# Layer 1's result turned by VectorE and stored in runs of 512 bytes, with the tokens of a block reordered, in a two-layer attention kernel

## The chip, the cores and the metric

The kernel runs on one core of a Trainium2 chip. The metric is the device time of one execution in microseconds (us); lower is better. Engines are named as the profile names them: PE (TensorE, matmuls), PEld (its weight loads), DVE (VectorE), ACT (ScalarE), POOL (GpSimd), SP (SyncE, which issues nearly all DMAs here).

## What is computed

The input x has 4 batches of 128 channels and 64 x 64 = 4096 positions, in fp32. Layer 0 is attention over the positions of a group-normalised x, with a gate and a projection, added to x. Layer 1 treats each position as a token of 128 channels: self attention with one shared projection for queries and keys, added to the tokens, and then a batch-normalised linear map that drives a recurrence over the tokens. Cut to what matters:

```python
# layer 0 (per batch; q and k have 64 rows, v and gate 128)
attn = softmax(q.T @ k * SCALE);  x = x + proj((v @ attn.T) * gate)
# layer 1
t = to_tokens(x)                                  # [B, 4096, 128]
q = ln(t) @ W;  t = t + softmax(q @ q.T) @ ln(t)
wx = batchnorm(ln(t) @ Wf.T)
y[:, i] = sigmoid(wx[:, i] + y[:, i-1] @ V.T)     # along the tokens
x = from_tokens(t + y)                            # back to [B, 128, 4096]
```

Softmax is a sum over all keys, so tokens may be kept in any order inside a block as long as scores, values and results agree on it. The recurrence and the output need them in their natural order.

## The kernel before

All work is in `fast`; `general` is another path, taken only if a check on the device fails at the end, and it isn't taken here. Batches run one after the other. A batch's 4096 tokens are 8 blocks (NB) of 512 (QB), and a block is 4 tiles (NQ) of 128 tokens.

**Layer 0** (`layer0`, run by `attention`): for each query block, 16 pairs of key tiles; TensorE makes scores (L223), ScalarE the exponential e (L225), VectorE adds e into acc for the denominators (L230, L232), and TensorE multiplies with v (L403), two pairs behind (LAG). The e tiles rotate through 4 buffers. When a block is through, `finish` queues small steps in `pending`: `sums`, `denominators`, `projection`, `tokens`, with `nothing` as empty places. The attention loop takes one step of `pending` every so many iterations, or one of `ahead` (the next batch's norms and projections), so that these steps lie between the matmuls.

Layer 0 has channels on the partitions and layer 1 has tokens there. `move` (L255) makes that turn: VectorE transposes 32x32 blocks (L261) into d, one DMA writes d (256 KB) to a DRAM scratch turn_d (L264), and four DMAs of 64 KB read it back (L266) so that the 32x32 blocks land where a full transpose has them. There are three moves in a block: x with the bias (tile t), the projected attention (yt), and the normalised tokens h (qt).

**Layer 1** (`layer1`): the score matrix is symmetric, since queries and keys are the same. For each block n (order 6, 7, 5, 4, ... 0) only blocks a <= n are computed: scores (L672), exponentials with row sums into slots (L678), and products with h (L539, in `direct`). For a < n the exponentials are also turned, by VectorE (L683) into dd and by 16 DMAs of 64 KB per pair of blocks (L710) into tt, and used four iterations later for block a (L552 in `reversed_products`), whose row sums DVE takes at L557. In the last batch the pair of blocks 1 and 0 isn't turned: block 0 computes block 1's scores itself, in the order given by `order`. `count` counts a block's parts and calls `finish` when they are complete; its limit is one lower for blocks 0 and 1 of the last batch.

`finish` (L579) loads the stored tokens (L599) and queues: `tokens` (the attention result oacc transposed on TensorE L608, scaled and added on DVE L610 to give t1, layernorm L276 to L280, with 1/sqrt on GpSimd L131, L132, to give h2), `result` (t1 transposed on TensorE L621, copied by ScalarE L624, stored to t2_d L625), two empty places, `turn` (h2 transposed on TensorE L630, copied by ScalarE L631 to th), `inputs` (the linear map L635, its statistics L636, and a copy L639 or L642). In the last batch's blocks 0 to 3 there are no empty places, and block 0's `tokens` goes to the head of the queue. These steps share one PSUM bank (ps_m).

**The scan** at the end: t2 loads all four t2_d (L776); the recurrence runs over pieces of 32 tokens with 12 tokens of warm-up, 44 steps in all, each with two matmuls (L823), two sigmoids (L827) and preloads (L810); the results are added to t2 (L837) and stored (L842).

The program's instructions are put in order on each engine by the framework's scheduler, so the order on the chip is near the order of the code but not the same.

Of the kernel before, what the change touches and what calls it, by code (L numbers as in the profile page):

```python
# [18 lines left out]
P = 128  # L19
B, C, N = 4, 128, 4096  # L20
# [9 lines left out]
QB = 512  # L30
NB = N // QB
# [18 lines left out]
def conv_attn_hybrid_kernel(  # L50
# [17 lines left out]
    turn_d = [dram.tile([P, 4, NQ, 32], F32, name=f"turn{i}_d") for i in range(8)]  # L68
    t2_d = dram.tile([B, C, N], F32, name="t2_d")
    wx_d = dram.tile([B, C, N], F32, name="wx_d")  # L70

# [86 lines left out]
def fast(  # L158
# [13 lines left out]
    with ExitStack() as st:  # L172
# [79 lines left out]
                nc.tensor.matmul(m[:, r, :cols], lhsT=lhsT[rs], rhs=rhs[rs], start=True, stop=True)  # L252
            return m[:, 0, :cols], m[:, 1, :cols]

        def move(blocks, dst):  # L255

            nonlocal n_moves
            d = work.tile([P, 4, NQ, 32], F32, tag="d", name="d", bufs=2)  # L260
            nc.vector.transpose(d.rearrange("q a j i -> q j a i"), blocks)  # L261
            via = turn_d[n_moves % len(turn_d)]
            n_moves += 1
            nc.sync.dma_start(via, d)  # L264
            for a in range(4):
                nc.sync.dma_start(dst[bass.ts(a, 32)], via[:, a].rearrange("(p i) j k -> i p j k", p=4))  # L266

        n_moves = 0

# [15 lines left out]
        def tiles(t):  # L285

            return [t[:, :, j, :] for j in range(NQ)]

        def quarters(t):
            return [t[:, j, :].rearrange("q (p i) -> q p i", p=4) for j in range(NQ)]  # L290
# [97 lines left out]
        def layer0(b, gate, q, k, v, need):  # L388
            h = big.tile([P, NT, C], F32, tag="h", name="h")
            qt = big.tile([P, N], F32, tag="qt", name="qt")  # L390

            def score_mm(n, p, half):
                r = bass.ts(half, DQ)
                return k[r, bass.ts(p, P)], q[r, bass.ts(n, QB)]

            def weigh(o, n, p, e):

                if o is None:
                    o = [ps_o.tile([P, QB], F32, tag="o", name=f"o{r}") for r in range(2)]
                for h in range(2):  # L400
                    for r in range(2):
                        rs = bass.ts(r, DQ)
                        nc.tensor.matmul(  # L403
                            o[r], lhsT=v[rs, p + h * PAIRS, :], rhs=e[rs, h, :],
                            start=(p == 0 and h == 0), stop=(p == PAIRS - 1 and h == 1),
                        )
                return o

            def finish(n, o, acc):
                cs, ts = bass.ts(n, QB), bass.ts(n, NQ)  # L410
                og = work.tile([P, QB], F32, tag="og", name="og")
# [10 lines left out]
                sub = stat.tile([P, NQ, 4], F32, tag="sub", name="sub", bufs=2)  # L422

                def sums():


                    half, blocks = acc[:, 0, :], acc[:, 1, :]
                    nc.vector.tensor_tensor(half, half, blocks, ALU.add)
                    nc.vector.transpose(blocks, half)
                    nc.vector.tensor_reduce(  # L430
                        sub, blocks.rearrange("q (j f k) -> q j f k", j=NQ, f=4), AX.X, ALU.add
                    )
                    move(xb.rearrange("c (j f k) -> c j f k", j=NQ, f=4), t)

                def denominators():
                    m0, m1 = halves(quart, sub.rearrange("q j f -> q (j f)"))
                    tot = stat.tile([P, NQ, 4], F32, tag="tot", name="tot", bufs=2)
                    flat = tot.rearrange("q j f -> q (j f)")
                    nc.vector.tensor_copy(flat, m0)
                    nc.vector.tensor_tensor(flat, flat, m1, ALU.add)  # L440
                    nc.vector.tensor_tensor(
                        tot, tot,
                        own.rearrange("q (j f) -> q j f", j=1).to_broadcast([P, NQ, 4]), ALU.mult,
                    )
                    den = den_all[:, b * NT + n * NQ : b * NT + (n + 1) * NQ]
                    nc.vector.tensor_reduce(den, tot, AX.X, ALU.add)
                    nc.vector.reciprocal(rinv, den)

                def projection():
                    m0, m1 = halves(wt["ps"], og)  # L450
                    nc.scalar.copy(og, m1)
                    nc.vector.tensor_tensor(og, m0, og, ALU.add)
                    move(og.rearrange("c (j f k) -> c j f k", j=NQ, f=4), yt)

                def tokens():
                    for j in range(NQ):
                        nc.vector.scalar_tensor_tensor(  # L457
                            t[:, :, j, :], yt[:, :, j, :], rinv[:, j : j + 1], t[:, :, j, :],
                            ALU.mult, ALU.add,
                        )  # L460
                    nc.sync.dma_start(t_d[b, n], t)
                    layernorm(tiles(t), quarters(h[:, ts, :]))

                    move(
                        h[:, ts, :].rearrange("q j (p i) -> q j p i", p=4),
                        qt[:, cs].rearrange("c (p j k) -> c p j k", j=NQ, p=4),
                    )
                    done.add((b, n))

                pending.extend([sums, nothing, denominators, projection, nothing, tokens])  # L470

            attention(score_mm, None, SCALE, weigh, finish, need)
            return h, qt

        def layer1(b, h, qt):
# [52 lines left out]
            def order(n):  # L528


                return [0, 1] if b == B - 1 and n == 0 else list(range(n, -1, -1))

            def turns(n, a):
                return a < n and not (b == B - 1 and n == 1)
# [37 lines left out]
            def count(n):  # L572


                parts[n] += 1
                if parts[n] == NB - (b == B - 1 and n < 2):
                    finish(n)

            def finish(n):  # L579
# [3 lines left out]
                if b == B - 1 and n == 0:  # L583

                    one, two = (ep.tile([P, 2, QB], F32, tag="e", name="last") for _ in range(2))
                    h2, t1 = (one[:, r, :].rearrange("q (j c) -> q j c", j=NQ) for r in range(2))
                    th, t2 = two[:, 0, :], two[:, 1, :]

                    def bank():
                        return ps_s.tile([P, 2, QB], F32, tag="s", name="ml")[:, 0, :]  # L590
                else:
                    h2 = work.tile([P, NQ, C], F32, tag="h2", name="h2")
                    th = work.tile([P, QB], F32, tag="th", name="th")
                    t1 = work.tile([P, NQ, C], F32, tag="og", name="t1b")
                    t2 = None

                    def bank():
                        return ps_m.tile([P, QB], F32, tag="m", name="m1")
# [16 lines left out]
                    layernorm(quarters(t1), quarters(h2))  # L615

                def result():
                    nonlocal t2
                    m = bank()
                    for j in range(NQ):  # L620
                        nc.tensor.transpose(m[:, bass.ts(j, P)], t1[:, j, :], ident)  # L621
                    if t2 is None:
                        t2 = work.tile([P, QB], F32, tag="xb", name="t2")
                    nc.scalar.copy(t2, m)  # L624
                    nc.sync.dma_start(t2_d[b, :, cs], t2)  # L625

                def turn():
                    m = bank()
                    for j in range(NQ):
                        nc.tensor.transpose(m[:, bass.ts(j, P)], h2[:, j, :], ident)  # L630
                    nc.scalar.copy(th, m)  # L631

                def inputs():
                    m = bank()
                    nc.tensor.matmul(m, lhsT=wt["f"], rhs=th, start=True, stop=True)  # L635
# [8 lines left out]

                if b == B - 1 and n == 0:
                    pending.appendleft(tokens)
                    pending.extend([result, turn, inputs])
                elif b == B - 1 and n < 4:
                    pending.extend([tokens, result, turn, inputs])
                else:  # L650
                    pending.extend([tokens, result, nothing, nothing, turn, inputs])


            for n in [NB - 2, NB - 1] + list(range(NB - 3, -1, -1)):
# [4 lines left out]
                for a in order(n):  # L659
# [4 lines left out]
                    for i in range(2):  # L664
# [588 lines left out]
```

## Time and profile before

| | us |
|---|---|
| three runs | 3066.79, 3070.16, 3072.19 |
| median | 3070.16 |
| the profiled execution | 3067.95, its span 3066.1 |
| PE busy | 3000.1 (98%) |
| DVE busy | 1882.3 (61%) |
| ACT busy | 1154.7 (38%) |
| POOL busy | 148.3 (5%) |
| DMA packets | 233171, 241 MB |

How to read the profile: a group's line gives source line, engine, operation, output and inputs with the shape, the count, then the busy us in total and the mean ns of one, and behind the last bar the idle time of the engine just before these instructions and what ended it. The chain of waits is the work that ended last, followed back from the end. The granted TensorE clock was full (mean 0.994) but for the first microseconds and the stretch between attention and scan.

### The profile page before, as it was taken

The numbers are of one execution on the slowest core, as the hardware profiler recorded it, in microseconds if no ns is written. First come the engines' busy times: TensorE is split into PE (matmuls) and PEld (weight loads), VectorE is DVE, ScalarE is ACT, GpSimd is POOL, SyncE is SP. The second block draws the span as 40 slices with busy tenths as digits, with TensorE's granted clock in tenths as the row PEclk, the third lists the DMA queues.
The fourth block names the chain that finished last, engine by engine and source line by source line (L and its number), as shares of the span: only waits on it lengthen the run. The fifth ranks groups of instructions, "written<-read, shape, count | busy, mean of one in ns | idle before, by whom it ended". The sixth has DMA issues, their size and how long they took to land.

```text
span 3066.1 us, 32642 instructions
## 1 busy us (share of the span) xinstructions
PE 3000.1 (98%) x10834; PEld 1377.5 (45%) x10834; DVE 1882.3 (61%) x3160; ACT 1154.7 (38%) x2148; POOL 148.3 (5%) x187
## 2 busy tenths in 40 slices
PE   7999999999999999999999999999999999999996
PEld 3444444444444444444444444444444444444443
DVE  6666665655666666655567666655566666455556
ACT  3444433333344443333344443333334444323334
POOL 0000000000000000000000000000000000000000
PEclk9999999999999999999999999999999999999998
DMA  1011143433211123333311113333321112543333
GB/s 52 28 56 56 42 115 86 99 93 92 53 56 55 41 82 96 93 96 92 85 46 61 39 50 112 88 96 93 94 61 52 46 49 90 139 104 93 99 111 159
DMA packets 233171, 241.17 MB, mean 79 GB/s; under 512 B 88480, under 2 KB 144288, under 8 KB 231968
## 3 DMA queue, kind: packets, MB, share of 16 engines
q1 hardware_dynamic: 231984, 238.18, 27.8%
q8 instruction: 89, 1.46, 0.2%
q14 instruction: 90, 0.74, 0.1%
q10 hardware_dynamic: 1008, 0.79, 0.1%
HBM read 65.80 MB, written 56.62 MB: 40 GB/s over the span
## 4 chain that ended last, share of the span: by engine, by line
PE 95%; DVE 3%; ACT 1%; POOL 0%; DMA 0%; issue 0%; ACTq 0%; SPq 0%; DVEq 0%; POOLq 0%
PE o L403 29%; PE o L539 16%; PE ps L223 15%; PE ps L672 14%; PE ot L552 12%; PE m L252 1%; PE m L635 1%; PE mq L497 1%; PE ps L505 1%; PE mp L335 1%; PE mp L370 1%; PE mp L355 1%; DVE ps_r L810 1%; DVE t2s L837 1%; PE m L630 1%; PE m L608 0%
## 5 line engine op out<-in xcount | busy, mean ns | idle before, releaser
L403 PE MATMUL o<-e,nxt 64*128 64x512 f32 x4096 | 964.8, 590 | 0.0
L225 ACT ACTIVATE e<-ps 128x1024 f32<-128x1024 f32 x512 | 521.6, 1025 | 678.2 <-PE ps L223 653.2
L232 DVE TENSOR_TENSOR acc<-acc,e 128x1024 f32<-128x1024 f32 x448 | 547.6, 1222 | 237.4 <-ACT e L225 221.6
L403 PEld LDWEIGHTS o<-e,nxt 64*128 64x128 f32 x4096 | 399.6, 187 | 483.4 <-issue 475.1
L678 ACT ACTIVATE e<-ps,shift 128x512 f32<-128x512 f32 x516 | 350.4, 683 | 670.0 <-PE ps L672 506.1
L539 PE MATMUL o<-e,h 128*128 128x512 f32 x1160 | 539.5, 592 | 0.0
L223 PE MATMUL ps<-nxt 64*128 64x512 f32 x2048 | 535.8, 597 | 2.2 <-ACT e L225 2.2
L672 PE MATMUL ps<-qt 128*128 128x512 f32 x1032 | 490.9, 595 | 2.9 <-ACT qt L498 2.7
L552 PE MATMUL ot<-tt,h 128*128 128x512 f32 x888 | 399.5, 592 | 0.0
L683 DVE STREAM_TRANSPOSE dd<-e 128x512 f32<-128x512 f32 x444 | 287.2, 687 | 87.9 <-ACT e L678 75.3
L539 PEld LDWEIGHTS o<-e,h 128*128 128x128 f32 x1160 | 218.3, 190 | 266.5 <-issue 261.9
L223 PEld LDWEIGHTS ps<-nxt 64*128 64x128 f32 x2048 | 194.4, 187 | 231.2 <-issue 158.9
L672 PEld LDWEIGHTS ps<-qt 128*128 128x128 f32 x1032 | 187.8, 190 | 213.0 <-issue 188.0
L552 PEld LDWEIGHTS ot<-tt,h 128*128 128x128 f32 x888 | 168.0, 190 | 209.5 <-issue 206.8
L557 DVE TENSOR_REDUCE slots<-tt 128x4 f32<-128x2048 f32 x111 | 250.8, 2260 | 9.8 <-DMA tt<-dd 9.2
L566 DVE TENSOR_TENSOR oacc<-oacc,ot 128x512 f32<-128x512 f32 x87 | 59.7, 686 | 187.0 <-PE ot L552 186.9
L131 POOL TENSOR_SCALAR rstd<-mv 128x4 f32<-128x4 f32 x64 | 14.5, 227 | 2429.7 <-DVE mv L277 2429.7
L678 ACT ACTIVATION_READ_ACCUMULATOR e<-ps,shift 128x1 f32 x516 | 101.3, 196 | 0.0
L457 DVE SCALAR_TENSOR_TENSOR t<-yt,rinv,t 128x128 f32<-128x128 f32 x128 | 36.6, 347 | 71.1 <-DMA yt<-turn_d 71.1
L420 POOL TENSOR_SCALAR xb<-xb,bpc 128x512 f32<-128x512 f32 x32 | 60.9, 1904 | 321.0 <-DMA xb<-in_x_dram 311.3
L132 POOL TENSOR_TENSOR rstd<-rstd,mhalf 128x4 f32<-128x4 f32 x64 | 66.4, 1037 | 5.3
L280 DVE TENSOR_SCALAR h<-t,mv,rstd 128x128 f32<-128x128 f32 x128 | 35.7, 344 | 47.0 <-POOL rstd L132 47.0
(160 smaller groups left out, 1659.5 us busy)
## 6 DMA issues: line engine op xcount, KB each, us to landing
tt<-dd SPq DMA_DIRECT2D x1776, 64.0 KB, 2.0
turn_d<-d SPq DMA_DIRECT2D x96, 256.0 KB, 2.0
t_d<-t SPq DMA_DIRECT2D x63, 256.0 KB, 2.0
nxt<-in_x_dram SPq DMA_DIRECT2D x16, 512.0 KB, 5.6
xb<-in_x_dram SPq DMA_DIRECT2D x32, 256.0 KB, 2.9
t<-turn_d SPq DMA_DIRECT2D x128, 64.0 KB, 2.0
yt<-turn_d SPq DMA_DIRECT2D x128, 64.0 KB, 2.0
qt<-turn_d SPq DMA_DIRECT2D x128, 64.0 KB, 2.1
```

The source lines that it names most:

```text
L132: nc.gpsimd.tensor_tensor(dst, dst, mhalf[:, :n], ALU.pow)
L223: nc.tensor.matmul(ps[:, h, :], lhsT=lhsT, rhs=rhs, start=True, stop=True)
L225: nc.scalar.activation(e, ps, AF.Exp, scale=scale)
L232: nc.vector.tensor_tensor(acc, acc, e, ALU.add)
L403: nc.tensor.matmul(o[r], lhsT=v[rs, p + h * PAIRS, :], rhs=e[rs, h, :], start=(p == 0 and h == 0), stop=(p == PAIRS - 1 and h == 1),)
L420: nc.gpsimd.tensor_scalar(xb, xb, bpc, None, ALU.add)
L539: nc.tensor.matmul(o, lhsT=h[:, NQ * a + 2 * i + half, :], rhs=e[:, half, :], start=(a == order(n)[0] and i == 0 and half == 0), stop=(a = ...
L552: nc.tensor.matmul(ot, lhsT=h[:, NQ * n + j, :], rhs=t[:, :, j, :, :].rearrange("q p k j -> q k p j"), start=(j == 0), stop=(j == NQ - 1),)
L557: nc.vector.tensor_reduce(slots[:, bass.ts(n, NQ), a], t.rearrange("q p b k j -> q b p (k j)"), AX.XY, ALU.add,)
L672: nc.tensor.matmul(ps[:, half, :], lhsT=qt[:, bass.ts(at, P)], rhs=qt[:, bass.ts(n, QB)], start=True, stop=True,)
L678: nc.scalar.activation(e[:, half, :], ps[:, half, :], AF.Exp, bias=shift, accum_out=slots[:, at, n : n + 1],)
L683: nc.vector.transpose(d.rearrange("q f b k j -> q k b f j")[:, 2 * i + half], e[:, half, :].rearrange("q (b f j) -> q b f j", b=NQ, f=NQ),)
```

## The change

- The order of tokens inside a block of layer 1 is another one. Tile j's partition (f, k) holds token 128f + 32j + k of the block, where it was token 128j + 32f + k. `sums`, `denominators` and `projection` follow (views `f j k` for `j f k`), and `inputs` reads th through a permuted view that puts the tokens in their natural order.
- `move` becomes `turn_out` and a read: VectorE's transpose as before, then four DMAs of 64 KB write it to DRAM in runs of 512 bytes, each from 32 partitions; the scratch turn_d then has the finished layout [128, 512], and one DMA of 256 KB reads it.
- `result` uses `turn_out` to store t1 to t2_d: a DVE transpose and four DMAs take the place of four TensorE transposes, the ScalarE copy and one DMA. It is no longer a step of its own in `pending`; `turn` calls it at its end.
- In the last batch, block 0 takes its parts in the order [1, 0] instead of [0, 1], and a part for block 1 is counted when its scores for it are issued, so block 1's `finish` is called then instead of earlier. The limits of `count` follow.

```diff
-        def move(blocks, dst):
+        def turn_out(blocks, dst):
             d = work.tile([P, 4, NQ, 32], F32, tag="d", name="d", bufs=2)
             nc.vector.transpose(d.rearrange("q a j i -> q j a i"), blocks)
+            for f in range(4):
+                nc.sync.dma_start(
+                    dst.rearrange("(a i) m -> i a m", a=4)[:, :, bass.ts(f, P)],
+                    d[bass.ts(f, 32)].rearrange("i a j k -> i a (j k)"),
+                )
+
+        def move(blocks, dst):
+            nonlocal n_moves
             via = turn_d[n_moves % len(turn_d)]
             n_moves += 1
-            nc.sync.dma_start(via, d)
-            for a in range(4):
-                nc.sync.dma_start(dst[bass.ts(a, 32)], via[:, a].rearrange("(p i) j k -> i p j k", p=4))
+            turn_out(blocks, via)
+            nc.sync.dma_start(dst, via)
...
-                return [0, 1] if b == B - 1 and n == 0 else list(range(n, -1, -1))
+                return [1, 0] if b == B - 1 and n == 0 else list(range(n, -1, -1))
...
-                if parts[n] == NB - (b == B - 1 and n < 2):
+                if parts[n] == NB - (b == B - 1 and n == 0):
                     finish(n)
...
                 def result():
-                    nonlocal t2
-                    m = bank()
-                    for j in range(NQ):
-                        nc.tensor.transpose(m[:, bass.ts(j, P)], t1[:, j, :], ident)
-                    if t2 is None:
-                        t2 = work.tile([P, QB], F32, tag="xb", name="t2")
-                    nc.scalar.copy(t2, m)
-                    nc.sync.dma_start(t2_d[b, :, cs], t2)
+                    turn_out(t1.rearrange("q j (p i) -> q j p i", p=4), t2_d[b, :, cs])
...
                     nc.scalar.copy(th, m)
+                    result()
...
-                    nc.tensor.matmul(m, lhsT=wt["f"], rhs=th, start=True, stop=True)
+                    natural = th.rearrange("c (j p k) -> c p j k", j=NQ, p=4)
+                    nc.tensor.matmul(m, lhsT=wt["f"], rhs=natural, start=True, stop=True)
...
-                    pending.extend([result, turn, inputs])
+                    pending.extend([turn, inputs])
                 elif b == B - 1 and n < 4:
-                    pending.extend([tokens, result, turn, inputs])
+                    pending.extend([tokens, turn, inputs])
                 else:
-                    pending.extend([tokens, result, nothing, nothing, turn, inputs])
+                    pending.extend([tokens, nothing, nothing, turn, inputs])
...
-                            if a == n and i == 0:
+                            if a == order(n)[0] and i == 0:
                                 direct()
+                        if a > n and i == 1:
+                            count(a)
```

More of the change, by code (lines that the diff above doesn't have):

```diff
@@ L66, in conv_attn_hybrid_kernel @@
     t_d = dram.tile([B, NB, P, 4, NQ, 32], F32, name="t_d")
-    turn_d = [dram.tile([P, 4, NQ, 32], F32, name=f"turn{i}_d") for i in range(8)]
+    turn_d = [dram.tile([P, QB], F32, name=f"turn{i}_d") for i in range(8)]
     t2_d = dram.tile([B, C, N], F32, name="t2_d")
@@ L253, in halves @@
             return m[:, 0, :cols], m[:, 1, :cols]
+        def turn_out(blocks, dst):
+            d = work.tile([P, 4, NQ, 32], F32, tag="d", name="d", bufs=2)
+            nc.vector.transpose(d.rearrange("q a j i -> q j a i"), blocks)
+            for f in range(4):
[3 more added lines that the diff above has]
+                )
         def move(blocks, dst):
             nonlocal n_moves
-            d = work.tile([P, 4, NQ, 32], F32, tag="d", name="d", bufs=2)
-            nc.vector.transpose(d.rearrange("q a j i -> q j a i"), blocks)
             via = turn_d[n_moves % len(turn_d)]
             n_moves += 1
-            nc.sync.dma_start(via, d)
-            for a in range(4):
-                nc.sync.dma_start(dst[bass.ts(a, 32)], via[:, a].rearrange("(p i) j k -> i p j k", p=4))
+            turn_out(blocks, via)
+            nc.sync.dma_start(dst, via)
         n_moves = 0
@@ L287, in tiles, with flat @@
             return [t[:, :, j, :] for j in range(NQ)]
+        def flat(t):
+            return t.rearrange("q p j i -> q (p j i)")
         def quarters(t):
@@ L420, in finish @@
                 nc.gpsimd.tensor_scalar(xb, xb, bpc, None, ALU.add)
-                sub = stat.tile([P, NQ, 4], F32, tag="sub", name="sub", bufs=2)
+                sub = stat.tile([P, 4, NQ], F32, tag="sub", name="sub", bufs=2)
                 def sums():
@@ L430, in sums @@
                     nc.vector.tensor_reduce(
-                        sub, blocks.rearrange("q (j f k) -> q j f k", j=NQ, f=4), AX.X, ALU.add
+                        sub, blocks.rearrange("q (f j k) -> q f j k", j=NQ, f=4), AX.X, ALU.add
                     )
-                    move(xb.rearrange("c (j f k) -> c j f k", j=NQ, f=4), t)
+                    move(xb.rearrange("c (f j k) -> c j f k", j=NQ, f=4), flat(t))
                 def denominators():
[L436 to L440, printed above, removed]
+                    m0, m1 = halves(quart, sub.rearrange("q f j -> q (f j)"))
+                    tot = stat.tile([P, 4, NQ], F32, tag="tot", name="tot", bufs=2)
+                    both = tot.rearrange("q f j -> q (f j)")
+                    nc.vector.tensor_copy(both, m0)
+                    nc.vector.tensor_tensor(both, both, m1, ALU.add)
                     nc.vector.tensor_tensor(
                         tot, tot,
-                        own.rearrange("q (j f) -> q j f", j=1).to_broadcast([P, NQ, 4]), ALU.mult,
+                        own.rearrange("q (f j) -> q f j", j=1).to_broadcast([P, 4, NQ]), ALU.mult,
                     )
                     den = den_all[:, b * NT + n * NQ : b * NT + (n + 1) * NQ]
-                    nc.vector.tensor_reduce(den, tot, AX.X, ALU.add)
+                    nc.vector.tensor_reduce(den, tot.rearrange("q f j -> q j f"), AX.X, ALU.add)
                     nc.vector.reciprocal(rinv, den)
@@ L452, in projection @@
                     nc.vector.tensor_tensor(og, m0, og, ALU.add)
-                    move(og.rearrange("c (j f k) -> c j f k", j=NQ, f=4), yt)
+                    move(og.rearrange("c (f j k) -> c j f k", j=NQ, f=4), flat(yt))
                 def tokens():
@@ L462, in tokens @@
                     layernorm(tiles(t), quarters(h[:, ts, :]))
[L464 to L467, printed above, removed]
+                    move(h[:, ts, :].rearrange("q j (p i) -> q j p i", p=4), qt[:, cs])
                     done.add((b, n))
@@ L586, in finish @@
                     h2, t1 = (one[:, r, :].rearrange("q (j c) -> q j c", j=NQ) for r in range(2))
-                    th, t2 = two[:, 0, :], two[:, 1, :]
+                    th = two[:, 0, :]
                     def bank():
@@ L594, in finish @@
                     t1 = work.tile([P, NQ, C], F32, tag="og", name="t1b")
-                    t2 = None
                     def bank():
```

## The prediction

> **What bounds the kernel now.** I read the page first: busy shares and the chain of work that ended last.
>
> ```profile
> span 3066.1 us, 32642 instructions
> ...
> PE 3000.1 (98%) x10834; PEld 1377.5 (45%) x10834; DVE 1882.3 (61%) x3160; ACT 1154.7 (38%) x2148; POOL 148.3 (5%) x187
> ...
> PE 95%; DVE 3%; ACT 1%; POOL 0%; DMA 0%; issue 0%; ACTq 0%; SPq 0%; DVEq 0%; POOLq 0%
> ```
>
> TensorE is busy for 98% of the span and holds 95% of the chain; no queue or DMA holds 1%. So an instruction taken off TensorE should shorten the span by what it holds, and work on another engine costs only where TensorE comes to wait for it. Next the groups of instructions, shapes kept apart, for the step that is moved (busy us, mean ns; then the engine's idle time before them):
>
> ```profile
> L261 DVE STREAM_TRANSPOSE d<-h 128x512 f32<-128x512 f32 x32 | 22.8, 711 | 1.1
> ...
> L621 PE MATMUL m<-ident,t1b 128*128 128x128 f32 x124 | 18.9, 275 | 0.0
> ...
> L624 ACT COPY t<-m 128x512 f32<-128x512 f32 x31 | 18.1, 584 | 56.0 <-PE m L621 51.5 <-issue 4.6
> ```
>
> TensorE never waited before L621 (idle 0.0): its 124 transposes (4 more, of the very last block, have a row of their own) cost array time and no wait. How much is not the 275 ns, because matmuls overlap. TensorE's timeline (start, us, group) gives it:
>
> ```profile
> 2952.27 0.60 PE L621 MATMUL m<-ident,t1b 128*128 128x128 f32 x4
> 2952.71 1.02 PE L672 MATMUL ps<-qt 128*128 128x512 f32 x2
> ...
> 2961.13 0.60 PE L608 MATMUL m<-ident,oacc 128*128 128x128 f32 x4
> 2961.57 3.60 PE L539 MATMUL o<-e,h 128*128 128x512 f32 x8
> 2965.00 0.60 PE L621 MATMUL m<-ident,t1b 128*128 128x128 f32 x4
> ```
>
> From the start of four transposes to the start of what follows is 2952.71 - 2952.27 = 0.44 us. Attention ends when the last L539 is through, at 2965.00. From there the bound changes: a serial stretch leads to the scan. The chain of waits there (start, us):
>
> ```profile
> 2965.75 0.85 DVE h L280 x3
> 2966.61 0.61 DVE oacc L566
> ...
> 2967.26 0.66 PE ml L608 x4
> ...
> 2971.43 1.05 POOL rstd L132
> ...
> 2972.90 1.11 PE ml L630 x4
> 2974.03 0.59 ACT last L631
> ...
> 2974.67 2.09 PE ml L635 x2
> ```
>
> Here VectorE carries the end: block 0's last sum (oacc) starts only when block 1's layernorm output h is done. The sigmoid that opens the scan starts at 2982.20.
>
> **What the Trainium skill says.** "Trainium Kernel Development and Optimization", Performance Expectations, calls matmul busy time a bad metric because matmuls are pipelined. The trace agrees: 0.60 us stand in the row where 0.44 us pass, so I price TensorE by distances between starts. "VectorE: DVE Perf Modes", The three transpose paths, says that VectorE turns 32x32 blocks only and writes SBUF, where TensorE turns 128x128 into PSUM. So the full turn must be finished by the addresses of the DMA, which is what the stores do; L261 has this operation at 711 ns for 128x512. "DMA: Bandwidth & Descriptors", Specifications, puts line rate at 512 B or more. Before, the runs through turn_d are 512 B on reading; after, on writing. No row shows a store in such runs.
>
> **The change part by part.**
>
> 1. *Result off TensorE.* 32 x 4 transposes go. 30 of the 32 groups start before 2965.00: 30 x 0.44 = **13.2 us** off TensorE's stream. The other two (blocks 1 and 0 of the last batch) lie beside VectorE's work in the serial stretch: nothing. The 32 copies L624 free ScalarE of 32 x 0.584 = 18.7 us; at 38% busy that is no time of the span.
>
> 2. *Turned by VectorE.* 32 transposes of 0.711 us, 22.8 us more. In a window of layer 1 (500 to 740 us) VectorE is busy 138 of 240 us, so it is hidden there. But the compiled order puts the transpose ahead of the layernorm's last aggregation, so GpSimd's 1/sqrt and the output h come 0.64 us later (start to start of such a transpose and what follows, at 137.13 and 137.77). The L630 transposes wait for h: the chain from t1 to h is 1.04 + 1.21 + 0.64 + 1.47 + 1.03 = 5.4 us. Between tokens and turn lie two empty slots, and one iteration of layer 1 (two score and two direct products) is 4 x 0.86 = 3.44 us: hidden. Only blocks 1 to 3 of the last batch have no slot between; there it may cost 0 to 1 us each, and I take nothing since the order again puts other products between.
>
> 3. *Moves.* Before: one 256 KB write, then four 64 KB reads; after: four 64 KB writes, then one 256 KB read, so five SP issues either way. In one block the write issued at 126.68, the reads at 128.71, and VectorE went on with yt at 132.23: 5.55 us. After: four issues of 0.43 (1.73 us in that block), 2.0 to land, 0.34 to issue the read, 2.9 to 3.0 to land (rows xb and t of 256 KB): about 7.0 us, 1.4 more. If a store of 512 B pieces landed at 3.0 it would be 2.4 more; at 1.8, the shortest 64 KB read, 1.2. VectorE waits in order: behind its L457 stand the acc adds L232, and ScalarE's exponentials wait for those through the four e buffers. In that block the e buffer written at 142.62 had been freed by an add that ended at 138.95, 3.7 us earlier. So 1.4 us is hidden: nothing.
>
> 4. *The store's issues.* 1 becomes 4 per block on SP, 96 more, at 0.33 to 0.63 us each. The L710 transfers queue behind them, and L552 waits for those.
>
> ```profile
> 572.44 10.00 SPq L710 DMA_DIRECT2D tt<-dd  x16
> 586.67 0.33 SPq L625 DMA_DIRECT2D t_d<-t  x1
> ```
>
> SP issues 16 in 10.0 us, and L552 groups start 12.9 us apart (593.61, 606.49, 619.43): some 2.9 us free per turn, against at most 4 x 0.63 - 0.33 = 2.2 us once per several turns. Also SP stood 142.2 us at L625 waiting for ScalarE's copy, a wait that an early VectorE transpose mostly takes away. Nothing.
>
> 5. *The last batch's end.* Block 1 is now complete only when block 0's scores for it exist. In the compiled order its four L608 transposes come after the last direct product, not before: 0.44 us more off the stream, and its whole token step lands in the serial stretch. From the last product's end (0) on VectorE: oacc 0.2 to 0.8; t1 of block 1 to 1.84; stats with the transpose among them 1.21 + 0.64, to 3.69; 1/sqrt 1.47, to 5.16; h to 6.2; three of block 0's scaled adds to 6.97. Block 1's turn on TensorE and ScalarE brings its bn_st to 8.3, through at 8.95, and the last aggregation to 9.05; 1/sqrt to **10.5**, where block 0's normalise starts. Before, that was 2972.50 - 2965.00 = 7.5: **3.0 us longer**. From there the chain is the same 9.7 us to the scan; block 0's own transpose fits where VectorE waited 2.05 us for L635. Bounds: 0 (if engines overlap as before) to 6.
>
> 6. *Orders of tokens.* L635 reads a permuted operand as L497 does: 599 against 610 ns, so nothing (62 x 11 ns = 0.7 us either way). sums and denominators keep instructions and sizes.
>
> Sum: -13.2 - 0.44 + 3.0 = **-10.6 us**, on the profiled span 3055.5. That execution took 3067.95, inside the runs' 3066.79 to 3072.19; from their median 3070.16 the forecast is **3059.6 us**.
>
> **The rivals.**
>
> *The gain is mostly given back.* The serial stretch grows by 6 instead of 3, blocks 1 to 3 hold TensorE up 1 us each, and the scan waits up to 2 us for t2s: its loads issued at 2976.82, took up to 22.4, and were first used at 3002.3, 3.1 us of margin, while block 0's store now ends some 3 us later than before. That is -13.6 + 6 + 3 + 2 = -2.6: 3067.6, no change. For it: VectorE and GpSimd take turns in that stretch. Against: L630 waited only 1.8 us in all before.
>
> *SP's queue becomes the bound in layer 1 (slower).* If nothing of the store's 2.2 us per block were hidden, that is 32 x 2.2 = 70 us; the point where it decides is 10.6 / 32 = 0.33 us per block getting through to L552. With a third getting through, +23 - 10.6: 3082.6. For it: SP is 78% taken (10.0 of 12.9 us). Against: L552 waited for tt only 2.4 us in all, and SP's 142.2 us wait falls away.
>
> *More is gained.* The serial stretch does not grow: -13.6, 3056.6.
>
> That the change does not do what it says is excluded by the compiled order: no L621 left, stores of 32x4x128.
>
> **How the numbers follow.** A measurement here tells about 0.2% (6.1 us) from no change: faster is below 3064.0, slower above 3076.3. Forecast 0.70 (3056 to 3063), more gained 0.12, given back 0.12, SP 0.06: faster 0.82, same 0.12, slower 0.06. The range, 3055.0 to 3066.5, takes in the tail's bounds, the blocks' waits, the runs' own scatter of 2.7 us and the nearer half of the give-back.
>
> **What would show it.** Right: PE's busy time down by about 19 us with L621's rows gone, L683 and L232 counts unchanged, the last direct product 13 to 14 us earlier, and 10 to 11 us instead of 7.5 from there to block 0's normalise. Wrong: L552 or L630 waiting for DMA or VectorE by more than some us in total, ScalarE's L225 waiting longer for acc than the 13.6 us of now, or the scan waiting for t2s. A slower landing than 3 us of the 64 KB stores would break step 3 first.

## The result, and the profile after

The changed kernel takes **3080.92 us** (median of 4 runs, 3079.55 to 3082.70) against 3069.86 us (3066.79 to 3072.19) beside it: a ratio of 1.0037, 95% interval 1.0020 to 1.0054. It is slower by 11 us where 10.6 us less were forecast. The profiled spans, 3078.5 and 3066.1 us, differ by 12.4 us; the sum of the prediction had said 3055.5, so 23.0 us are to be explained.

The page of the kernel after:

```profile
span 3078.5 us, 32596 instructions
...
PE 2998.1 (97%) x10706; PEld 1366.2 (44%) x10706; DVE 1890.5 (61%) x3192; ACT 1136.3 (37%) x2116; POOL 149.3 (5%) x187
...
PE 90%; DVE 3%; SPq 2%; ACT 1%; DMA 1%; issue 1%; POOL 1%; DVEq 0%; ACTq 0%
```

The 128 records of L621 are gone, yet PE's busy time fell by 2.0 us, not by some 19. The profile models the ends of matmuls, so stalls can hide in that sum; and TensorE's share of the chain fell from 95% to 90%. The groups, shapes kept apart, show where idle time appeared: first two of the kernel before, then the same two (now L628 and L613) and VectorE's new transposes in the kernel after.

```profile
L630 PE MATMUL m<-ident,h 128*128 128x128 f32 x124 | 21.1, 283 | 2.2 <-DVE h L280 1.8
...
L608 PE MATMUL m<-ident,oacc 128*128 128x128 f32 x124 | 19.9, 275 | 0.0
```

```profile
L628 PE MATMUL m<-ident,h 128*128 128x128 f32 x124 | 25.8, 300 | 8.7 <-DVE h L286 8.6
...
L613 PE MATMUL m<-ident,oacc 128*128 128x128 f32 x124 | 21.2, 277 | 4.5 <-DVE wx L642 4.1
...
L260 DVE STREAM_TRANSPOSE d<-t1b 128x512 f32<-128x512 f32 x31 | 21.1, 680 | 0.1
```

VectorE's new transposes take about what was forecast (0.680 us each, for 0.711). But TensorE is now idle for 8.7 us ahead of turn's transposes, 8.6 of them until h is there, where it was 2.2 us; and for 4.5 us ahead of the next block's tokens, where it was 0.0. Idle time is only a part of it: span less busy grew by 14.4 us in all (80.4 against 66.0), the end included, while 23.0 us are to be explained. So I counted stalls from the trace: for each pair of successive matmuls the distance of their starts less the array time of the first. For the array time I took the distance at which such matmuls usually follow each other: 0.429 us for 512 columns, half of it with 64 rows (these start in pairs, 0.43 us from pair to pair), a quarter (0.107) for 128 columns. The sum runs from nine tenths through layer 0 of one batch to the same place in the next. This is my calculation, not a view; it repeats from batch to batch within some tenths.

| kernel | us per batch | stalls in it |
|---|---|---|
| before | 733.0 | 11.4 |
| after | 735.1 to 735.4 | 17.0 to 17.2 |

8 x 0.44 = 3.5 us of transposes left each batch, as forecast, and 5.6 us of stalls came: +2.1. Sorted by the matmul that starts late, 2.1 us of the 5.6 stand ahead of turn's transposes and 1.8 ahead of the tokens'; the rest is spread over scores and products. Three such batches hold 17.0 us of the 23.0. Matched one by one, products of layer 0 inside a batch keep a constant distance between the two kernels (-0.1 us through the first batch's, +2.0 through the second's): nothing was lost where the moves are. The loss is in layer 1. The rest: 2.8 us of stalls in the last batch, which ends attention at 2971.16 instead of 2965.00, and 3.2 us more than forecast from there to the end (107.3 against 101.1 us).

TensorE's timeline in the kernel after, at the end of the first layer 1, shows a stall as it is read:

```profile
749.83 5.71 PE L672 MATMUL ps<-qt 128*128 128x512 f32 x12
755.37 1.00 PE L628 MATMUL m<-ident,h 128*128 128x128 f32 x4
756.21 1.03 PE L511 MATMUL ps<-qt 128*128 128x256 f32 x4
757.07 1.10 PE L635 MATMUL m<-th,w 128*128 128x512 f32 x2
759.55 0.66 PE L613 MATMUL m<-ident,oacc 128*128 128x128 f32 x4 [1.38 <-DVE wx L642]
760.05 3.61 PE L558 MATMUL ot<-tt,h 128*128 128x512 f32 x8
```

The same steps in the kernel before:

```profile
751.03 0.60 PE L630 MATMUL m<-ident,h 128*128 128x128 f32 x4
751.47 2.74 PE L672 MATMUL ps<-qt 128*128 128x512 f32 x6
754.05 3.60 PE L552 MATMUL ot<-tt,h 128*128 128x512 f32 x8
757.48 1.88 PE L539 MATMUL o<-e,h 128*128 128x512 f32 x4
759.20 1.02 PE L635 MATMUL m<-th,w 128*128 128x512 f32 x2
760.06 1.02 PE L672 MATMUL ps<-qt 128*128 128x512 f32 x2
760.91 1.88 PE L539 MATMUL o<-e,h 128*128 128x512 f32 x4
762.63 0.60 PE L608 MATMUL m<-ident,oacc 128*128 128x128 f32 x4
```

In the kernel after, twelve score matmuls stand in a row, then turn, inputs (L635) and the next block's tokens (L613) nearly back to back. All three use the one bank of ps_m, so L613 waits 1.38 us until VectorE has copied the inputs out of it, and the eight products L558 stand behind it. In the kernel before, eighteen matmuls stand between turn and inputs and six between inputs and the next tokens, and nothing waits.

### The profile page after: what moved, and what is told of

Read it like the earlier page. It is cut to its first block, busy times and chain, and to the rows that moved or that the text cites. A ratio compares the mean times of both kernels' runs of the same rounds, so it can differ in the third digit from the quotient of the medians.

```text
span 3078.5 us, 32596 instructions
## 1 busy us (share of the span) xinstructions
PE 2998.1 (97%) x10706; PEld 1366.2 (44%) x10706; DVE 1890.5 (61%) x3192; ACT 1136.3 (37%) x2116; POOL 149.3 (5%) x187
## 4 chain that ended last, share of the span: by engine, by line
PE 90%; DVE 3%; SPq 2%; ACT 1%; DMA 1%; issue 1%; POOL 1%; DVEq 0%; ACTq 0%
PE o L412 28%; PE o L545 15%; PE ps L223 15%; PE ps L672 12%; PE ot L558 11%; SPq L712 2%; PE m L252 1%; PE m L635 1%; PE mq L503 1%; PE mp L344 1%; PE mp L379 1%; PE ps L511 1%; PE m L628 1%; DVE t2s L839 1%; PE mp L364 1%
## 5 line engine op out<-in xcount | busy, mean ns | idle before, releaser
L678 ACT ACTIVATE e<-ps,shift 128x512 f32<-128x512 f32 x516 | 350.3, 683 | 670.3 <-PE ps L672 405.2
L558 PE MATMUL ot<-tt,h 128*128 128x512 f32 x888 | 400.4, 593 | 0.0
L558 PEld LDWEIGHTS ot<-tt,h 128*128 128x128 f32 x888 | 167.0, 190 | 206.5 <-issue 204.0
L678 ACT ACTIVATION_READ_ACCUMULATOR e<-ps,shift 128x1 f32 x516 | 101.3, 196 | 0.0
L466 DVE SCALAR_TENSOR_TENSOR t<-yt,rinv,t 128x128 f32<-128x128 f32 x128 | 36.5, 347 | 81.8 <-DMA yt<-turn_d 81.8
L523 ACT ACTIVATE e<-ps,shift 128x256 f32<-128x256 f32 x64 | 29.8, 470 | 119.7 <-PE ps L517 119.6
```

The costliest lines, as they stand in the source:

```text
L558: nc.tensor.matmul(ot, lhsT=h[:, NQ * n + j, :], rhs=t[:, :, j, :, :].rearrange("q p k j -> q k p j"), start=(j == 0), stop=(j == NQ - 1),)
L678: nc.scalar.activation(e[:, half, :], ps[:, half, :], AF.Exp, bias=shift, accum_out=slots[:, at, n : n + 1],)
```

## The experiments

Each kernel was timed beside the kernel before, whose medians were 3068.6 to 3069.3 us. After each group of kernels a table gives the time, its ratio to the kernel before, and the us and stalls per batch as counted above.

**First: a lost slot, VectorE or SP?** My first theory was that the step taken out of the queue had kept tokens and turn apart. Its rivals were VectorE's transpose and the stores on SP.

*a_spacer*, one empty step more:

```diff
-                    pending.extend([tokens, nothing, nothing, turn, inputs])
+                    pending.extend([tokens, nothing, nothing, nothing, turn, inputs])
```

(likewise one `nothing` for blocks 1 to 3 of the last batch)

> The changed kernel with one empty step more between tokens and turn (three instead of two, in the last batch one instead of none); all work as in the changed kernel. Lost slot (the removed step had also kept tokens and turn, and one block's inputs and the next block's tokens, apart): the 5.6 us of new TensorE waits per batch at the end of layer 1 mostly go, three to four times 5.6, so about 3062 to 3066 us; the end after the last direct product stays 5 us longer than before. VectorE's transpose or SP's stores at fault: nothing changes, 3078 to 3083.

*a_step*, the result as a step of its own again (in the last batch's blocks 0 to 3 too):

```diff
                     nc.scalar.copy(th, m)
-                    result()
...
-                    pending.extend([tokens, nothing, nothing, turn, inputs])
+                    pending.extend([tokens, result, nothing, nothing, turn, inputs])
```

> The changed kernel with the result's turn by VectorE as a step of its own where it stood before (tokens, result, two empty steps, turn, inputs), the last batch too. Lost slot: as with the empty step, 3062 to 3066 us. VectorE's transpose at fault: no gain, since the transpose stands as close behind the layernorm as before, 3078 to 3083. SP's stores at fault: 3078 to 3083.

*b_noslot*, the kernel before with its result in turn's step:

```diff
                     nc.scalar.copy(th, m)
+                    if not (b == B - 1 and n < 4):
+                        result()
...
-                    pending.extend([tokens, result, nothing, nothing, turn, inputs])
+                    pending.extend([tokens, nothing, nothing, turn, inputs])
```

> The kernel before, with the result's TensorE transposes called at the end of turn instead of in a step of their own, except for blocks 0 to 3 of the last batch; no VectorE transpose, old moves, old end. Lost slot: TensorE keeps its 13.2 us of transposes and gets the new waits of three batches and most of the fourth, about 3 x 5.6 = 17 us more, 3082 to 3090. VectorE's transpose or the stores at fault: as before, 3068 to 3072.

*a_unturned*, one plain store of t1; the turn of the result is left out:

```diff
-                    turn_out(t1.rearrange("q j (p i) -> q j p i", p=4), t2_d[b, :, cs])
+                    nc.sync.dma_start(t2_d[b, :, cs], t1.rearrange("q j c -> q (j c)"))
```

> The changed kernel with layer 1's result stored as it is by one 256 KB transfer: neither the VectorE transpose of the result nor three of its four SP issues; the turn of the result is left out. Lost slot: the new waits stay, less at most what 0.64 us per block makes of them, 3074 to 3081. VectorE's transpose ahead of the 1/sqrt, or SP's four issues, at fault: the 5.6 us per batch and a part of the longer end go, 3056 to 3064.

| kernel | us (ratio, 95%) | us per batch | stalls |
|---|---|---|---|
| a_spacer | 3077.16 (1.0018 to 1.0038) | 735.9 to 736.6 | 17.7 to 18.4 |
| a_step | 3062.36 (0.9972 to 0.9988) | 731.4 to 731.5 | 13.2 to 13.3 |
| b_noslot | 3084.13 (1.0036 to 1.0063) | 737.1 to 737.2 | 15.2 to 15.6 |
| a_unturned | 3060.76 (0.9958 to 0.9980) | 730.9 | 12.7 |

No theory fits all four. The lost slot explains a_step and b_noslot, but an empty slot instead of the step took no stall out of the batches (they grew; what it gained lies behind them, where its end is 2.8 us shorter), and leaving out the transpose and three stores brought nearly all.

**Second: transpose or stores, and the new end.** *a_onestore* keeps VectorE's transpose and stores d by one transfer, without placing its 32x32 pieces (`nc.sync.dma_start(t2_d[b, :, cs], d.rearrange("q a j i -> q (a j i)"))`).

> The changed kernel with the result turned by VectorE as there, but stored by one 256 KB transfer straight from d; the placing of the 32x32 pieces is left out. SP's four issues at fault: the time is that of the unturned store, 3058 to 3063. VectorE's transpose at fault: the time stays that of the changed kernel, 3077 to 3083. Both in equal parts: about 3070.

*a_poolq* passes `nc.gpsimd` as the queue of the result's four stores.

> The changed kernel with the four stores of the result issued by GpSimd instead of SP; nothing is left out. SP's issues at fault: 3058 to 3065, if GpSimd's 1/sqrt, which then stands behind stores, isn't held up. VectorE's transpose at fault: 3077 to 3083.

*a_step_oldtail* is a_step with the old end of the last batch:

```diff
-                return [1, 0] if b == B - 1 and n == 0 else list(range(n, -1, -1))
+                return [0, 1] if b == B - 1 and n == 0 else list(range(n, -1, -1))
...
-                if parts[n] == NB - (b == B - 1 and n == 0):
+                if parts[n] == NB - (b == B - 1 and n < 2):
...
-                        if a > n and i == 1:
-                            count(a)
```

> The result as a step of its own after tokens (3062.4 us with the new end of the last batch) with the old end: block 0 in the order [0, 1], block 1 complete without waiting for block 0's scores. If the new end costs what the profile of the changed kernel shows, 5.0 us from the last direct product to the first matmul of the scan, less the 0.44 us of transposes that come back: about 3058, and 3057 to 3060. If that lengthening belonged to the wider order of the last batch and not to the new end: 3061 to 3064.

*b_newtail* makes the reverse of that edit in the kernel before.

> The kernel before with the new end of the last batch alone (order [1, 0], block 1 counted when block 0's scores for it are issued), result still on TensorE. The new end costs 4 to 5 us: 3073 to 3075. The end costs nothing by itself: 3068 to 3071.

| kernel | us (ratio, 95%) | us per batch | stalls |
|---|---|---|---|
| a_onestore | 3058.61 (0.9954 to 0.9979) | 730.5 | 12.4 |
| a_poolq | 3069.27 (0.9998 to 1.0015) | 732.4 to 732.9 | 14.2 to 14.7 |
| a_step_oldtail | 3062.88 (0.9974 to 0.9988) | 731.4 to 731.6 | 13.2 to 13.4 |
| b_newtail | 3068.99 (0.9992 to 1.0009) | 733.0 to 733.1 | 11.4 to 11.5 |

VectorE's transpose costs nothing here, as predicted, and neither does the new end: in both pairs of kernels with the old and the new end the times agree, so it doesn't cost the 4 to 5 us that were thought possible. With one store the loss is gone. So three more issues on SP per block seem to cost 4.6 us per batch. GpSimd's queue gave back only about half (3069.27 us, where 3058 to 3065 were expected), a miss.

**Third: the number of issues and their place.** *b_four* splits the store of the kernel before:

```diff
-                    nc.sync.dma_start(t2_d[b, :, cs], t2)
+                    for f in range(4):
+                        fs = bass.ts(f, P)
+                        nc.sync.dma_start(t2_d[b, :, cs][:, fs], t2[:, fs])
```

> The kernel before, its result still turned by TensorE, with the one 256 KB store of a block split into four of 64 KB on SP (512 B pieces), as in the changed kernel. If three more issues per block on SP cost by themselves what they cost in the changed kernel (735.1 against 730.5 us per batch, 4.6 us more), TensorE's stalls rise by the same and the time is 3083 to 3090. If they cost only together with the lost step: 3068 to 3074.

*a_later* puts the four stores of the changed kernel's result under `with tc.high_priority(-500):`, which lowers their priority.

> The changed kernel with its four stores of the result at a lower priority in the scheduler, so that transfers to tt that are due at that time are issued ahead of them; same instructions. If what costs is that the stores stand ahead of transfers to tt: 3058 to 3065. If four issues cost wherever they stand on SP: 3077 to 3083.

*a_deferred* stores d by one transfer and leaves the placing to the loads ahead of the scan:

```diff
+    t2b_d = dram.tile([B, NB * 4, 32, 4, P], F32, name="t2b_d")
...
+                    nc.sync.dma_start(
+                        t2_d[b, 4 * n : 4 * n + 4].rearrange("f i a m -> (f i) (a m)"),
+                        d.rearrange("q a j k -> q (a j k)"),
+                    )
...
-            nc.sync.dma_start(t2[:, b, :], t2_d[b])
+            for a in range(4):
+                nc.sync.dma_start(
+                    t2[bass.ts(a, 32), b, :].rearrange("i (f m) -> i f m", m=P),
+                    t2_d[b, :, :, a, :].rearrange("f i m -> i f m"),
+                )
```

(inside this function t2_d is then the new t2b_d)

> The changed kernel with one 256 KB store per block of the result as VectorE left it, and the pieces put in place by the loads ahead of the scan, 16 of 512 KB in runs of 512 B instead of 4 of 2 MB; nothing is left out. If SP's issues in layer 1 are what costs: batches of 730.5 us as with one store, 3057 to 3062. If the loads come late for the scan: a wait of VectorE for t2s and up to 3068.

*a_deferred_step* adds a_step's edit to it.

> The same with the result as a step of its own after tokens. If the step's slot is worth something beside the issues: below the kernel without it, 3052 to 3057. If one issue leaves nothing to gain for the slot: the same within 3 us, 3056 to 3062.

| kernel | us (ratio, 95%) | us per batch | stalls |
|---|---|---|---|
| b_four | 3076.10 (1.0015 to 1.0034) | 735.7 | 14.0 |
| a_later | 3095.44 (1.0072 to 1.0100) | 740.8 to 741.0 | 22.6 to 22.8 |
| a_deferred | 3058.29 (0.9956 to 0.9980) | 730.6 | 12.4 |
| a_deferred_step | 3051.54 (0.9931 to 0.9958) | 728.2 | 10.0 to 10.1 |

a_deferred_step leaves nothing out and is faster than both kernels. But a_later is a clear miss: with some transfers to tt issued ahead of the stores the kernel is slower by 15 us than the changed one. And the waits of the changed kernel (first) and of the kernel before speak against SP (engine, tile and line, what it waited for, us in total, times, longest):

```profile
PE m L628 <- DVE h L286: 8.6, 13, 3.9
...
DVE slots L563 <- DMA tt<-dd: 7.3, 3, 4.7
...
PE m L613 <- DVE wx L642: 4.1, 3, 1.4
...
PEld ot L558 <- DMA tt<-dd: 2.2, 7, 0.8
```

```profile
DVE slots L557 <- DMA tt<-dd: 9.2, 3, 6.3
...
PEld ot L552 <- DMA tt<-dd: 2.4, 10, 0.2
...
PE m L630 <- DVE h L280: 1.8, 3, 0.6
```

The changed kernel, with four stores per block, waits for tt no longer than the kernel before with one (7.3 and 2.2 us against 9.2 and 2.4). In b_four these waits are 14.8 and 3.1 us, so this reading alone doesn't clear SP. What grew in the changed kernel are waits of TensorE for VectorE. Such waits depend on the order in which the scheduler writes the instructions, and that order had changed. a_deferred and the changed kernel have the same instructions on the four compute engines; compared place by place, another instruction stands at 708 of TensorE's 5545 places, 414 of VectorE's 3192, 70 of ScalarE's 1476 and 3 of GpSimd's 183 (an instruction that moves also shifts those that it passes). In the traces of b_four and of the kernel before, 773 of TensorE's 10834 records, 149 of VectorE's 3160 and 86 of ScalarE's 2148 differ in the same way.

**Fourth: SP or the order.** Each of these kernels keeps its own instructions and takes the order of another on TensorE, VectorE, ScalarE and GpSimd. The order was read from the other's compiled program, as numbers of traced instructions per engine, and written in as edges that fix the order only:

```diff
+    for engine, code in ORDER.items():
+        mine = [i for i in traced if str(i.engine).split(".")[-1] == engine ...]
+        before = None
+        for k in array.array("H", zlib.decompress(base64.b85decode(code))):
...
+            if before is not None:
+                tc.add_manual_dep(
+                    mine[k], before.name,
+                    mybir.DependencyInfo(mybir.DependencyClass.NoSync, mybir.DependencyReason.DATA),
+                    reason="order",
+                )
+            before = mine[k]
```

SP's own order stays with the scheduler. after_pinned takes a_deferred's order, deferred_as_after the changed kernel's, a_step_pinned that of a_deferred_step, and b_four_pinned that of the kernel before. The traces show that the order was taken: each runs the sequence of the kernel that it follows on all four engines, but for 2 of VectorE's 3192 records in after_pinned and in a_step_pinned.

*after_pinned*: 

> The changed kernel, every instruction and all four stores per block as they are, but with the order of instructions on TensorE, VectorE, ScalarE and GpSimd that the scheduler gave the kernel with one store per block and the loads putting the pieces in place (3058.3 us); edges that fix the order alone, no waits. If the scheduler's order is what the issues cost: 3058 to 3062. If SP itself holds the transfers up: 3077 to 3083.

*deferred_as_after*: 

> The other way round: one store per block and the pieces put in place by the loads, in the order that the scheduler gave the changed kernel. If the order is what costs: 3076 to 3083. If SP's issues are: 3057 to 3061.

*a_step_pinned*: 

> The kernel with the result as a step and four stores (3062.4 us), in the order that the scheduler gave the one with the same step and one store (3051.5 us). If the order is what costs: 3051 to 3055. If SP's issues: 3060 to 3064.

*b_four_pinned*: 

> The kernel before with its store split into four (3076.1 us), in the order of the kernel before. If the order is what costs: 3068 to 3071. If SP's issues: 3074 to 3078.

| kernel | its own order | in the other's order (ratio, 95%) | us per batch | stalls |
|---|---|---|---|---|
| after_pinned | 3080.92 | 3059.54 (0.9961 to 0.9981) | 730.6 | 12.4 |
| deferred_as_after | 3058.29 | 3092.15 (1.0062 to 1.0089) | 735.1 to 735.4 | 17.0 to 17.2 |
| a_step_pinned | 3062.36 | 3050.99 (0.9930 to 0.9958) | 728.2 to 728.4 | 10.1 to 10.2 |
| b_four_pinned | 3076.10 | 3069.10 (0.9991 to 1.0007) | 733.0 | 11.4 |

Every kernel takes the stalls of the order that it was given, to some tenths of a us, and its count of stores doesn't matter. That settles it for the stalls in the batches: three more issues per block on SP cost nothing by themselves that these runs can tell, and the order costs all of it. b_four_pinned still waits 12.6 and 3.1 us for tt, at the time of the kernel before. TensorE's timeline in after_pinned, at the place shown above (here inputs are L641, tokens L619, scores L678):

```profile
750.15 1.02 PE L641 MATMUL m<-th,w 128*128 128x512 f32 x2
751.01 1.88 PE L678 MATMUL ps<-qt 128*128 128x512 f32 x4
752.73 3.60 PE L564 MATMUL ot<-tt,h 128*128 128x512 f32 x8
756.16 3.60 PE L551 MATMUL o<-e,h 128*128 128x512 f32 x8
759.60 0.60 PE L619 MATMUL m<-ident,oacc 128*128 128x128 f32 x4
```

Twenty matmuls now stand between inputs and the next tokens, and there is no wait. SP at this time in the kernel after, and then in after_pinned (start, us, count of transfers):

```profile
735.23 28.17 SPq L712 DMA_DIRECT2D tt<-dd  x32
763.51 2.02 SPq L262 DMA_DIRECT2D t_d<-d  x4
765.63 0.58 SPq L643 DMA_DIRECT2D wxs_d<-wx  x1
```

```profile
728.23 27.40 SPq L718 DMA_DIRECT2D tt<-dd  x32
755.73 2.02 SPq L268 DMA_DIRECT2D t_d<-d  x4
757.85 0.58 SPq L649 DMA_DIRECT2D wxs_d<-wx  x1
```

The four stores take the same 2.02 us of SP in both, between the same neighbours; one kernel is 21 us faster.

deferred_as_after missed its expectation upwards, by 9 us. Its stalls per batch are those forecast; the rest is at the end. Its waits:

```profile
PE m L642 <- DVE h L293: 8.6, 13, 3.9
...
DVE t2s L857 <- DMA t2s<-t2b_d: 8.2, 1, 8.2
...
DVE t2s L857 <- issue: 4.2, 1, 4.2
...
PE m L620 <- DVE wx L656: 4.1, 3, 1.4
```

The waits for h and wx are the changed kernel's, figure for figure. The 12.4 us for t2s come from the 16 loads, which SP issues over 41 us: in this order the first addition to t2s starts 26 us after the first load, in a_deferred 37 us after it, where nothing waits for them.

Why the scheduler writes these orders stays open; no run looked into it. What GpSimd's queue costs apart from the order (a_poolq) stays open as well.

## Why the prediction was wrong

**Step 1, the result off TensorE (-13.2): right.** Each batch lost 3.5 us of array time (8 groups of four transposes at 0.44 us), as forecast.

**Step 2, turned by VectorE ("hidden: nothing"): the operation right, the slots wrong.** The transpose costs nothing that shows (a_onestore keeps it at 730.5 us per batch, a_unturned without it takes 730.9). But I took the two empty places between tokens and turn as time on the chip, "one iteration of layer 1 is 3.44 us: hidden". The scheduler decides what stands between them: an empty step has no instruction, and adding one moved the stalls from 17.0 to as much as 18.4 us. Taking a step from the kernel before cost 4.1 us per batch (b_noslot).

**Step 3, the moves ("nothing"): right.** Layer 0 keeps a constant distance between the two kernels. VectorE waited 81.8 us for yt where it had waited 71.1, or 0.3 us more in a block where 1.4 were forecast, and TensorE didn't feel it.

**Step 4, the store's issues ("Nothing"): right for SP and wrong for the kernel.** With the slots of step 2 this is the term that failed. As far as SP goes the working (2.2 us of issue in 2.9 us of free time) is borne out: b_four_pinned has the four stores and the time of the kernel before, a ratio of 0.9991 to 1.0007. What I left out is that the same three issues lead to another order on the other engines: b_four in its own order has 2.6 us more of stalls per batch. The changed kernel gets 5.6 us more per batch from its issues and its lost step together. With the step back and four stores 1.8 of these remain (a_step, 13.2 against 11.4), with one store and no step 1.0 (a_onestore, 12.4), and with one store and the step there are 1.4 less than before (a_deferred_step, 10.0). The prediction had named the sign: TensorE's wait for h at turn, 1.8 us before, is 8.6 us, while the waits for tt and for acc did not grow.

**Step 5, the end (+3.0): half of it, and wrong in cause.** From the last direct product to the end the kernel took 6.2 us longer. From that product to block 0's normalise passed 11.8 us, for 10.5 forecast and 7.5 before: 4.3 of the 6.2. The chain of waits of the kernel after shows this stretch:

```profile
2971.97 1.12 DVE t1b L615 x4
...
2975.14 1.05 POOL rstd L132
...
2976.70 1.17 PE m L628 x4
...
2978.59 2.09 PE m L635 x2
...
2981.89 1.05 POOL rstd L132
...
2982.96 0.36 DVE last L286
```

Block 1's whole token step stands in the serial stretch, as forecast, and its h starts at 5.05 us after the product's end, near where the sum had it (5.16). The mis-sized term is block 1's L635: it takes 2.09 us here, where the granted clock is 0.50 (from 2977.13 to 2994.19), and took 1.12 at 2968.49, where it is 1.00. Before, the clock was at 0.50 only from 2974.30 to 2981.10. The same longer stretch takes in the 12 matmuls that first fill ps_r (5.46 us from 2988.83, against 4.32 before), and from their start to the first sigmoid that reads ps_r it is 0.5 us longer. The largest part of what is left, 0.9 us, comes after the last matmul of the program, and no run tells why.

The cause named, the new order of block 0's parts, isn't the cause: in b_newtail the normalise starts 7.49 us after the product, exactly as before, and in a_step_oldtail, with the old end, 10.3 us after it. In after_pinned, with the changed kernel's instructions, it starts 7.7 us after it. That block 1's step ends up there is the scheduler's order again.

**The rivals.** "SP's queue becomes the bound in layer 1" gave 3082.6, 1.7 us from what was measured, by a mechanism that after_pinned and b_four_pinned refute. A time that fits isn't evidence for its mechanism. "The change doesn't do what it says" was excluded too quickly: the compiled order was used to see where the removed and added instructions stand, and not how many of the others had moved.

In a good order the changed kernel takes 3059.5 us (after_pinned), 9.8 us below the kernel before, where 10.6 less were forecast. That the two are so near is partly luck: each batch lost 3.5 us of transposes, as forecast, but has 1.0 us more of stalls than in the kernel before, and its end is 2.9 us longer (104.0 against 101.1), of which only 0.2 come before block 0's normalise. Whether the kernel before would gain from another order wasn't tried.

## What to carry to other kernels

Where a scheduler writes the order, an edit has two prices: that of its instructions, and that of the order into which it throws all the others; here two orders of the same instructions lie 21 us apart in a kernel with 97 to 98% of TensorE busy, and in the better one the edit gained about 10. So count the moved instructions of every engine before trusting a sum of durations, and look for steps that share one buffer and have come to stand back to back. To tell the two prices apart, give the changed kernel the other order (or the other kernel the new one) by edges that fix the order alone: each of four such runs took the stalls per batch of the order it was given.

## What the runs showed beside

- A version faster than both: VectorE turns the result in a step of its own, one 256 KB store per block leaves the pieces as they are, and 16 loads of 512 KB with runs of 512 B place them: 3051.54 us, 17 us below the kernel before. Its page:

```profile
span 3047.0 us, 32511 instructions
...
PE 2982.1 (98%) x10706; PEld 1364.6 (45%) x10706; DVE 1896.3 (62%) x3192; ACT 1136.1 (37%) x2116; POOL 152.9 (5%) x187
```

  PE's busy time is 16.0 us below that of the changed kernel with the same count of matmuls: the part of the stalls that the page counts as busy. a_step_pinned reaches the same 3051 us with four stores.
- A 64 KB store in pieces of 512 B lands in 1.8 us (median of 384), below the 2.0 us taken in step 3; SP mostly issues four of them in 1.8 to 2.0 us.
